# Block 2's norm ahead of the context's masking, and a reordered opening, in a cross-attention and feed-forward kernel

## The chip, the cores and the metric

The kernel runs on one core of a Trainium2 chip. Its engines work at the same time, each through its own queue and in order: TensorE (PE, with weight loads listed as PEld), VectorE (DVE), ScalarE (ACT), GpSimd (POOL), and SyncE (SP), which issues most of the DMAs. [...] The metric is the time of one execution on the device in microseconds (us). Before the change the median of three runs is 1310.03 us (1309.79 to 1311.21).

## The reference, cut to what matters

There is one batch: 2048 rows of `x` with 256 features, a context of 1601 rows with 192 features, 16 heads of 64 and a feed-forward part whose weights are signs. Everything is float32.

```python
xn  = layer_norm(layer_norm(x)) * g_norm
q   = xn @ Wq;   k, v = split(context @ Wkv)
k, v = concat(null_kv[0], k), concat(null_kv[1], v)     # key 0 is the null key
sim = (q / 64**.25) @ (k / 64**.25).T                   # masked keys get -max
att = softmax(sim) @ v
x   = x + layer_norm(att @ Wout) * g_out
h   = relu(s0 * [u, -u] @ (+-1 of k0)) * 2              # u = layer_norm(x)
h   = relu(s1 * h @ (+-1 of k1)) * 2
out = x + s2 * h @ (+-1 of k2)
```

## The kernel before, in words

**Units.** The 2048 rows are four blocks of 512 (`b`), the heads eight pairs (`p`). A pair and a block are a unit `u`, 32 in all, pair by pair. A unit has three parts. In the first, 13 steps over chunks of 128 keys (`k`), PE makes scores with the keys on the partitions (`exps`, tile `sT`, L393); for `k` of 0 and 1 it adds minus the row maximum to them (L404), for later `k` it adds the scores with stepped keys (`kT` holds each chunk minus the one two before, `keys_stepped`), so that a tile turns from chunk to chunk. ACT takes the exponential into `e` (L406), and POOL adds the `e` up in `acc` (L621, L623). Between these steps PE and DVE make the row maxima of the next unit: `max_chunk` multiplies rounded queries and keys (`qr`, `kr`, L356), and DVE reduces them (L359). There are 12 chunks, numbered 3t + c (t a group of 128 rows, c one of three groups of 512 keys), and one for the remaining 66 keys (`REST`, L340 and L343). In the second part PE forms the weighted sums (`weighted`, tile `av`, L413, 52 matmuls) and, early in it, the denominators of the unit before (`divided`). In the third part, between units, ACT copies `av`; the maxima, combined by `max_combined` into `mcol` (L364), are turned by PE (`max_turned`, L369) and spread by DVE into `mT` (L371); the output projection of the unit before follows, the queries of the unit after the next (`project_q`, L213, with `qr` and `qT` made by ACT), and a quarter of the next pair's keys or values (`project_k`, `project_v`).

**Norm of the input.** For each block, `input_root` takes statistics on DVE (L77, L78) and the root on ACT (L443); `input_normed` takes the reciprocal and `nm`, the negated mean, on DVE (L447, L140), and then two ACT instructions a group of 128 rows (L143, L144) with `beside`, or DVE alone (L89); `input_turned` transposes on PE (L458, tile `xT`), and ACT and DVE write one half each of `xnT` (L459, L463; for block 1 both halves are ACT's). Blocks 0 and 1 are done in the opening, blocks 2 and 3 in units 0 and 1, between `max_combined` and the weighted sums (L642, L643). Only unit 0, just ahead of that, reloads half of `ctx_b` and multiplies both context tiles with the mask `keep` on DVE (L641): later pairs need them masked. Also in unit 0 DVE prepares the signs and scales of the feed-forward part (L665 to L669).

**The opening** (L468 to L578) is one list written out by hand, and each engine runs its part of it in that order. It has the loads, the norm of block 0, 40 idle matmuls (20 calls, 2 each) ahead of the first transposes, and for pair 0 the keys in four pieces (`first_keys`: matmuls L224 and L225; DVE masks them into `kT`, L227, and writes `kr` with the null key where the mask drops a key, L228), the values (`first_values`, two halves of matmuls, then a copy by ACT, L283), the first queries, the maxima of unit 0, the norm and turning of block 1, and the mask as a bias, `maskb` (L562, L563). The inverse mask `drop` is made on ACT (L530).

**PSUM.** There are two pools of two tiles, each tile two banks: `flex` and `spare`. In the opening and the feed-forward part `slot` takes from them alternately. A tile waits until the last reader of the one it replaces is done. DVE and ACT do not read one PSUM tile at the same time: at both places where they read `xT`, DVE begins when ACT is done.

**Feed-forward part.** After the last unit a block's rows go through three layers. Values are split into a rounded part `hi` (ACT) and the rest `lo` (DVE); `layer_pair` multiplies both with the same weights (L720), `first` and the loop of L774 drive it.

Of the kernel before, what the change touches and what calls it, by code (L numbers as in the profile page):

```python
# [36 lines left out]
def xattn_ffn(ctx, tc, x, ctxT, mask, g_norm, null_kv, wq, wkv, wout, g_out, k0, k1, k2, s0, s1, s2, out):  # L37
# [108 lines left out]
    with ExitStack() as att:  # L146
# [71 lines left out]
        def first_keys(n, get):  # L218

            kT, _, kr = pairs[0]  # L220
            start, w = CHUNKS[n]
            keys = ds(start, w)
            ps = get(f"psk_0_{n}")
            nc.tensor.matmul(ps[:, 0, :w], weights[0][1][:, 0, :], ctx_a[:, keys], start=True, stop=False)  # L224
            nc.tensor.matmul(ps[:, 0, :w], weights[0][2][:, 0, :], ctx_b[:, keys], start=False, stop=True)  # L225

            nc.vector.tensor_tensor(kT[:, keys], ps[:, 0, :w], keep[:, keys], ALU.mult)  # L227
            nc.vector.scalar_tensor_tensor(kr[:, keys], drop[:, keys], nullk[:, 0:1], kT[:, keys], ALU.mult, ALU.add)  # L228
            if n == 0:
# [148 lines left out]
        def rows_of(k):  # L378
            return 128 if k < KC - 1 else KLAST

        def exps(p, b, k, sT):

            kT, qT, mT = pairs[p][0], queries[p, b][0], shifts[p, b]
            n = rows_of(k)
            ps = sT[k % 2]  # L390
            for j in range(2):
                rows = ts(j, DH)
                nc.tensor.matmul(  # L393
                    ps[:n, j, :],
                    kT[rows, ds(128 * k, n)],
                    qT[rows, :],
                    start=k < 2,
                    stop=k >= 2,
                    skip_group_check=k >= 2,
                )  # L400
            if k < 2:
                for j in range(2):
                    rows = ts(j, DH)
                    nc.tensor.matmul(ps[:n, j, :], ones_r[rows, :n], mT[rows, :], start=False, stop=True)  # L404
            e = ep.tile([128, 2, 512], F32, tag="e", name=f"e_{p}_{b}_{k}")
            nc.scalar.activation(e[:n], ps[:n], AF.Exp, bias=maskb[:n, k : k + 1])  # L406
            return e
# [44 lines left out]
                centred(y_sb[:, 4 * b + j, :], x_sb[:, 4 * b + j, :], mv, r, j)  # L452

        def input_turned(b, get=flex):
            pt = get(f"xT_{b}")
            for j in range(4):
                for c in range(2):
                    nc.tensor.transpose(pt[:, c, ts(j, 128)], y_sb[:, 4 * b + j, ts(c, 128)], ident)  # L458
            nc.scalar.mul(xnT[:, b, 0, :], pt[:, 0, :], gn_sb[:, 0:1])  # L459
            if b == 1:  # L460
                nc.scalar.mul(xnT[:, b, 1, :], pt[:, 1, :], gn_sb[:, 1:2])
            else:
                nc.vector.tensor_scalar_mul(xnT[:, b, 1, :], pt[:, 1, :], gn_sb[:, 1:2])  # L463
# [64 lines left out]

        for keys in (ds(0, 512), ds(512, KEYS - 512)):
            nc.scalar.activation(drop[:, keys], keep[:, keys], AF.Identity, bias=ones[:, 0:1], scale=-1.0)  # L530
        input_normed(0, *xn)

        idle = slot("idle")
        for _ in range(20):
            nc.tensor.matmul(idle[:, 0, :128], ident, ident, start=True, stop=True)
        input_turned(0, slot)
        first_keys(0, slot)
        project_q(0, 0, slot)
        xn = input_root(1)
        first_keys(1, slot)  # L540
        input_normed(1, *xn, beside=True)

        nc.scalar.activation(warm, eps_sb, AF.Exp)

        max_chunk(0, 0, 0, slot)
        max_chunk(0, 0, 3, slot)
        first_keys(2, slot)
        max_chunk(0, 0, 6, slot)
        first_values(0, 0, slot)
        max_chunk(0, 0, 9, slot)  # L550
        first_values(0, 1, slot)
        max_chunk(0, 0, 1, slot)
        first_keys(3, slot)
        keys_stepped(0)
        first_values(1, 0, slot)
        max_chunk(0, 0, 4, slot)
        first_values(1, 1, slot)
        max_chunk(0, 0, 7, slot)
        input_turned(1, slot)
        max_chunk(0, 0, 10, slot)  # L560

        nc.vector.tensor_scalar(maskb[:, : KC - 1], mcol_u8[:, : KC - 1], -MASKED, MASKED, ALU.mult, ALU.add)  # L562
        nc.vector.tensor_scalar(  # L563
            maskb[:KLAST, KC - 1 : KC], mcol_u8[:KLAST, KC - 1 : KC], -MASKED, MASKED, ALU.mult, ALU.add
        )
        first_values(2, 0, slot)
        max_chunk(0, 0, 2, slot)
        first_values(2, 1, slot)
        max_chunk(0, 0, REST, slot)
        first_values(3, 0, slot)  # L570
        max_chunk(0, 0, 5, slot)
        project_q(0, 1, slot, 0)
        max_chunk(0, 0, 8, slot)
        max_chunk(0, 0, 11, slot)
        project_q(0, 1, slot, 1)
        max_combined(0, 0)
        max_turned(0, 0)
        begin.__exit__(None, None, None)  # L578
        last = None
        with tc.manual_schedule():  # L580
            for u, (p, b) in enumerate(units):
# [27 lines left out]
                for k in range(KC):  # L609
                    if k == 2 and last is not None:  # L610
                        nc.scalar.copy(seen[:, 1:2], last[3][:1, 0, 0:1])  # L611
                    if k == 0:

                        odd = spare(f"sT_{p}_{b}_1")
                        sT = [spare(f"sT_{p}_{b}_0"), odd]
                    es.append(exps(p, b, k, sT))
                    if nxt is not None:
                        max_chunk(*nxt, order[k])
                    m = rows_of(k)
                    if k == 1:  # L620
                        nc.gpsimd.tensor_tensor(acc, es[0], es[1], ALU.add)  # L621
                    elif k > 1:
                        nc.gpsimd.tensor_tensor(acc[:m], acc[:m], es[k][:m], ALU.add)  # L623
# [6 lines left out]
                if u == len(units) - 2:  # L630
                    norm_begin(0, y_sb, "y")
                    norm_root(0)
                    norm_end(0, y_sb, y_sb, beside=True)

                    nc.scalar.activation(warm, eps_sb, AF.Exp)
                if u == 0:


                    nc.sync.dma_start(out=ctx_b[64:, 1:], in_=ctxT[128:CD, :])
                    for part in (ctx_a, ctx_b):  # L640
                        nc.vector.tensor_tensor(part, part, keep, ALU.mult)  # L641
                if u < 2:  # L642
                    input_normed(u + 2, *input_root(u + 2), beside=True)  # L643
                    nc.scalar.activation(warm, eps_sb, AF.Exp)

                av = spare(f"av_{p}_{b}")
                for k in range(KC):
# [3 lines left out]
                if u in (len(units) - 4, len(units) - 3):  # L651
# [4 lines left out]
                    else:  # L656
# [57 lines left out]
    def layer_pair(b, n, g, out, w, parts, chunks):  # L714

        ps = slot(f"ps{n}_{b}_{g}")
        steps = [(c, part) for c in range(chunks) for part in range(2)]
        for i, (c, part) in enumerate(steps):
            for f in range(2):
                nc.tensor.matmul(  # L720
# [115 lines left out]
```

## Time and profile before

| | us |
|---|---|
| median of three runs | 1310.03 |
| the profiled execution's own time | 1309.9 |
| its span | 1308.1 |
| PE busy | 1290.2 |
| DVE busy | 819.7 |
| POOL busy | 997.9 |
| ACT busy | 624.7 |
| start of the first exponential | 39.21 |
| end of unit 0's weighted sums | 65.02 |
| start of unit 1's first scores | 80.64 |

The page gives the busy time of each engine, the span in 40 slices of 32.7 us (a digit is tenths), the chain of work that ended last, and groups of instructions by line. The list in order of time has a line for each stretch of equal instructions: its start, its duration, engine, line, the operation, `out<-in` with sizes, how many, and in brackets the idle time of the engine ahead of it with what ended that idle time. The table by stretches gives a stretch, its length, the busy time of PE, PEld, DVE, ACT and POOL with numbers of instructions, the granted clock of PE (1.00 is full), and the DMA's share and rate.

### The profile page before, as it was taken

How to read it: one execution, taken by the hardware profiler on the slowest of the kernel's cores; microseconds unless marked ns; L12 is line 12 of the kernel's file. 1: busy time of each engine (PE TensorE's matmuls, PEld its weight loads, DVE VectorE, ACT ScalarE, POOL GpSimd, SP SyncE). 2: the span in 40 equal slices, each digit the busy share in tenths (PEclk: the TensorE clock that was granted, in tenths of full speed). 3: DMA queues.
4: the chain of work that ended last, by engine and by line, in shares of the span. 5: the costliest groups of instructions: out<-in, count | busy, mean ns of one | idle time of the engine just before them, and what ended most of it. 6: DMA issues, size and time to landing. Idle time of an engine off the chain costs nothing.

```text
span 1308.1 us, 15963 instructions
## 1 busy us (share of the span) xinstructions
PE 1290.2 (99%) x6568; PEld 657.8 (50%) x6568; DVE 819.7 (63%) x822; ACT 624.7 (48%) x740; POOL 997.9 (76%) x503
## 2 busy tenths in 40 slices
PE   8989999999999999999999999999999999999998
PEld 6334444444444444444444444444444443688887
DVE  7877666666666666666666666666666784554431
ACT  4576444444444444454555555555555457321121
POOL 4768988898889888998889888988898999611100
PEclk9989999999999999999999999999999999999999
DMA  6100000000000000000000000000000010000000
GB/s 143 21 1 5 1 1 13 6 1 1 13 5 1 1 13 5 1 1 5 9 5 1 1 13 5 1 1 5 1 17 1 1 41 1 1 9 9 17 17 17
DMA packets 16122, 13.18 MB, mean 10 GB/s; under 512 B 2656, under 2 KB 15520, under 8 KB 16048
## 3 DMA queue, kind: packets, MB, share of 16 engines
q1 hardware_dynamic: 14928, 11.02, 3.2%
q8 instruction: 52, 0.85, 0.3%
q10 hardware_dynamic: 640, 0.79, 0.2%
q0 software_dynamic: 480, 0.34, 0.2%
q14 instruction: 22, 0.18, 0.0%
HBM read 10.04 MB, written 2.10 MB: 9 GB/s over the span
## 4 chain that ended last, share of the span: by engine, by line
PE 91%; DVE 3%; ACT 2%; POOL 2%; DMA 1%; issue 1%; SPq 0%; DVEq 0%; POOLq 0%; ACTq 0%
PE sT L393 28%; PE av L413 26%; PE ps L720 9%; PE max L356 7%; PE psq L213 4%; PE po L421 4%; PE ps L746 2%; PE den L431 2%; PE psv L298 2%; PE psk L238 2%; PE sT L404 1%; DVE mx L359 1%; POOL acc L623 1%; PE psv L310 1%; DMA x_sb<-in_x 1%; PE psk L243 1%
## 5 line engine op out<-in xcount | busy, mean ns | idle before, releaser
L623 POOL TENSOR_TENSOR acc<-acc,e 128x1024 f32<-128x1024 f32 (+1 forms) x352 | 847.0, 2406 | 27.6
L359 DVE TENSOR_REDUCE mx<-max 128x2 f32<-128x1024 f32 x384 | 452.0, 1221 | 81.4 <-PE max L356 81.3
L406 ACT ACTIVATE e<-sT,maskb 128x1024 f32<-128x1024 f32 (+1 forms) x416 | 459.6, 1113 | 42.0 <-PE sT L404 11.8
L393 PE MATMUL sT<-qT,kT 64*128 64x512 f32 (+1 forms) x1664 | 448.5, 612 | 0.8 <-ACT e L406 0.2
L413 PE MATMUL av<-e,v 128*64 128x512 f32 (+1 forms) x1664 | 369.5, 594 | 0.2 <-ACT e L406 0.2
L356 PE MATMUL max<-kr,qr 64*128 64x512 f32 x768 | 292.4, 750 | 0.0
L413 PEld LDWEIGHTS av<-e,v 128*64 128x64 f32 (+1 forms) x1664 | 116.7, 137 | 237.7 <-issue 222.6
L393 PEld LDWEIGHTS sT<-qT,kT 64*128 64x128 f32 (+1 forms) x1664 | 130.4, 181 | 153.6 <-ACT e L406 144.3
L671 ACT COPY avs<-av 128x512 f32<-128x512 f32 x32 | 18.7, 585 | 321.6 <-PE av L413 321.6
L433 DVE RECIPROCAL aoT<-den 128x512 f32<-128x512 f32 x31 | 104.0, 3356 | 60.0 <-PE den L431 60.0
L621 POOL TENSOR_TENSOR acc<-e,e 128x1024 f32<-128x1024 f32 x32 | 75.6, 2362 | 70.1 <-ACT seen L611 58.4
L356 PEld LDWEIGHTS max<-kr,qr 64*128 64x128 f32 x768 | 76.1, 187 | 90.4 <-DVE mx L359 68.4
L371 DVE TENSOR_TENSOR mT<-mt,pick 128x512 fp32r<-128x512 f32 x32 | 22.1, 691 | 119.0 <-PE mt L369 119.0
L720 PE MATMUL ps<-h0hi,w 128*128 128x512 f32 x256 | 79.6, 392 | 0.1
L720 PE MATMUL ps<-h0lo,w 128*128 128x512 f32 x256 | 78.9, 389 | 0.0
L122 POOL TENSOR_TENSOR y_sb<-y_sb,gout_sb 128x256 f32<-128x256 f32 x12 | 9.3, 776 | 88.8 <-DVE y_sb L89 88.8
L214 ACT ACTIVATE qr<-psq 128x512 fp32r<-128x512 f32 x32 | 19.1, 597 | 100.0 <-PE psq L213 97.1
L213 PE MATMUL psq<-xnT,wq 128*128 128x512 f32 x124 | 60.2, 609 | 2.5 <-DVE xnT L463 2.5
L709 DVE SCALAR_TENSOR_TENSOR h1lo<-ps,h1hi 128x1024 fp32r<-128x1024 f32 x16 | 19.6, 1224 | 68.3 <-ACT h1hi L708 68.2
L708 ACT ACTIVATE h1hi<-ps 128x1024 fp32r<-128x1024 f32 x16 | 16.4, 1025 | 95.0 <-PE ps L720 95.0
L421 PE MATMUL po<-wo,aoT 128*128 128x256 f32 x256 | 60.6, 379 | 0.0
L404 PE MATMUL sT<-mT,ones_r 64*128 64x512 f32 x128 | 52.3, 787 | 1.3 <-DVE mT L371 1.3
(157 smaller groups left out, 1060.9 us busy)
## 6 DMA issues: line engine op xcount, KB each, us to landing
out_x<-o SPq DMA_DIRECT2D x7, 256.0 KB, 2.1
x_sb<-in_x SPq DMA_DIRECT2D x3, 512.0 KB, 8.2
wa<-in_wkv SPq DMA_DIRECT2D x8, 128.0 KB, 2.7
wq<-in_wq SPq DMA_DIRECT2D x8, 128.0 KB, 2.2
wo<-in_wout SPq DMA_DIRECT2D x8, 128.0 KB, 2.0
xnT<-in_k SPq DMA_DIRECT2D x1, 1024.0 KB, 5.7
wb<-in_wkv SPq DMA_DIRECT2D x15, 64.0 KB, 2.4
ctx_a<-in_ctxT SPq DMA_DIRECT2D x2, 256.0 KB, 8.1
```

The source lines that it names most:

```text
L213: nc.tensor.matmul(ps[:, 0, :], weights[p][0][:, c, :], xnT[:, b, c, :], start=c == 0, stop=c == 1)
L356: nc.tensor.matmul(ps[:, j, :w], qr[rows, ts(t, 128)], kr[rows, ds(start, w)], start=True, stop=True)
L359: nc.vector.tensor_reduce(maxima[p, b][:, t, :, c], ps[:, :, :w], AX.X, ALU.max)
L393: nc.tensor.matmul(ps[:n, j, :], kT[rows, ds(128 * k, n)], qT[rows, :], start=k < 2, stop=k >= 2, skip_group_check=k >= 2,)
L404: nc.tensor.matmul(ps[:n, j, :], ones_r[rows, :n], mT[rows, :], start=False, stop=True)
L406: nc.scalar.activation(e[:n], ps[:n], AF.Exp, bias=maskb[:n, k : k + 1])
L413: nc.tensor.matmul(av[ts(j, DH), 0, :], v[:n, k, ts(j, DH)], e[:n, j, :], start=k == 0, stop=k == KC - 1)
L421: nc.tensor.matmul(pv[:, t, :], aoT[:, ts(t, 128)], weights[p][3], start=True, stop=True)
L433: nc.vector.reciprocal(aoT, ps)
L621: nc.gpsimd.tensor_tensor(acc, es[0], es[1], ALU.add)
L623: nc.gpsimd.tensor_tensor(acc[:m], acc[:m], es[k][:m], ALU.add)
L720: nc.tensor.matmul(ps[:, f, :], w(c)[:, ts(2 * g + f, 128)], parts[part][:, c, :], start=i == 0, stop=i == len(steps) - 1,)
```

## The change

The change has five parts.

1. Unit 0: the norm of block 2 (statistics, root, norm on ACT) stands ahead of the reload and the masking of the context. The sign operations move from unit 0 to unit 2.
2. Rounded keys: for all keys from 512 on, ACT writes the null key's part into `kr` once (one instruction over 1090 keys), and POOL adds `kT` to it piece by piece, where DVE made both in one instruction. `maskb` moves from DVE to POOL and to an earlier place.
3. Order of the opening: 17 calls of idle matmuls instead of 20; block 0's two halves of `xT` in two PSUM tiles; the chunks of maxima in twos; statistics of block 1 behind the third piece of keys, its norm behind chunk 9, the load of the Exp table behind chunk 4; the turning of block 1 behind chunk 10; three tiles near the end taken from a named pool.
4. First scores: `scores` is split from `exps`; unit 0's scores for `k` of 1 are issued ahead of the turning of the maxima, those for `k` of 0 behind it.
5. Feed-forward: in layer 0 the steps are sorted, all `hi` ahead of all `lo`.

```diff
@@ first_keys
-            nc.vector.scalar_tensor_tensor(kr[:, keys], drop[:, keys], nullk[:, 0:1], kT[:, keys], ALU.mult, ALU.add)
             if n == 0:
+                nc.vector.scalar_tensor_tensor(
+                    kr[:, keys], drop[:, keys], nullk[:, 0:1], kT[:, keys], ALU.mult, ALU.add
+                )
                 nc.vector.tensor_copy(kT[:, 0:1], nullk)
+            else:
+                nc.gpsimd.tensor_tensor(kr[:, keys], kr[:, keys].bitcast(F32), kT[:, keys], ALU.add)
@@ exps
-        def exps(p, b, k, sT):
+        def scores(p, b, k, ps):
...
+        def exps(p, b, k, sT):
+            mT = shifts[p, b]
+            n = rows_of(k)
+            ps = sT[k % 2]
+            if (p, b) != (0, 0) or k >= 2:
+                scores(p, b, k, ps)
@@ input_turned
             pt = get(f"xT_{b}")
+            pts = (pt, get("xT_0_1") if b == 0 else pt)
             for j in range(4):
                 for c in range(2):
-                    nc.tensor.transpose(pt[:, c, ts(j, 128)], y_sb[:, 4 * b + j, ts(c, 128)], ident)
-            nc.scalar.mul(xnT[:, b, 0, :], pt[:, 0, :], gn_sb[:, 0:1])
+                    nc.tensor.transpose(pts[c][:, c, ts(j, 128)], y_sb[:, 4 * b + j, ts(c, 128)], ident)
+            nc.scalar.mul(xnT[:, b, 0, :], pts[0][:, 0, :], gn_sb[:, 0:1])
...
@@ opening
+        nc.scalar.mul(pairs[0][2][:, 512:], drop[:, 512:], nullk[:, 0:1])
         input_normed(0, *xn)
         idle = slot("idle")
-        for _ in range(20):
+        for _ in range(17):
             nc.tensor.matmul(idle[:, 0, :128], ident, ident, start=True, stop=True)
         input_turned(0, slot)
         first_keys(0, slot)
         project_q(0, 0, slot)
-        xn = input_root(1)
         first_keys(1, slot)
-        input_normed(1, *xn, beside=True)
-        nc.scalar.activation(warm, eps_sb, AF.Exp)
+        nc.gpsimd.tensor_scalar(maskb[:, : KC - 1], mcol_u8[:, : KC - 1], -MASKED, MASKED, ALU.mult, ALU.add)
...
         max_chunk(0, 0, 0, slot)
         max_chunk(0, 0, 3, slot)
         first_keys(2, slot)
+        xn = input_root(1)
         max_chunk(0, 0, 6, slot)
+        max_chunk(0, 0, 9, slot)
+        input_normed(1, *xn, beside=True)
         first_values(0, 0, slot)
-        max_chunk(0, 0, 9, slot)
         first_values(0, 1, slot)
         max_chunk(0, 0, 1, slot)
+        max_chunk(0, 0, 4, slot)
+        nc.scalar.activation(warm, eps_sb, AF.Exp)
         first_keys(3, slot)
         keys_stepped(0)
         first_values(1, 0, slot)
-        max_chunk(0, 0, 4, slot)
+        max_chunk(0, 0, 7, slot)
         first_values(1, 1, slot)
-        max_chunk(0, 0, 7, slot)
+        max_chunk(0, 0, 10, slot)
         input_turned(1, slot)
-        max_chunk(0, 0, 10, slot)
-        nc.vector.tensor_scalar(maskb[:, : KC - 1], mcol_u8[:, : KC - 1], -MASKED, MASKED, ALU.mult, ALU.add)
...
         first_values(2, 0, slot)
         max_chunk(0, 0, 2, slot)
+        max_chunk(0, 0, REST, slot)
         first_values(2, 1, slot)
-        max_chunk(0, 0, REST, slot)
         first_values(3, 0, slot)
         max_chunk(0, 0, 5, slot)
-        project_q(0, 1, slot, 0)
-        max_chunk(0, 0, 8, slot)
-        max_chunk(0, 0, 11, slot)
-        project_q(0, 1, slot, 1)
+        max_chunk(0, 0, 8, flex)
+        project_q(0, 1, spare, 0)
+        max_chunk(0, 0, 11, flex)
+        project_q(0, 1, spare, 1)
         max_combined(0, 0)
+        odd = spare("sT_0_0_1")
+        sT = [spare("sT_0_0_0"), odd]
+        scores(0, 0, 1, sT[1])
         max_turned(0, 0)
+        scores(0, 0, 0, sT[0])
@@ units
+                if u < 2:
+                    input_normed(u + 2, *input_root(u + 2), beside=True)
+                    nc.scalar.activation(warm, eps_sb, AF.Exp)
                 if u == 0:
                     nc.sync.dma_start(out=ctx_b[64:, 1:], in_=ctxT[128:CD, :])
                     for part in (ctx_a, ctx_b):
                         nc.vector.tensor_tensor(part, part, keep, ALU.mult)
-                if u < 2:
-                    input_normed(u + 2, *input_root(u + 2), beside=True)
-                    nc.scalar.activation(warm, eps_sb, AF.Exp)
...
-                if u == 0:
+                if u == 2:
                     nc.vector.tensor_scalar(sgn, s_sb[:, 0:2], 0.0, None, ALU.is_ge)
@@ layer_pair
         steps = [(c, part) for c in range(chunks) for part in range(2)]
+        if n == 0:
+            steps.sort(key=lambda step: step[1])
```

More of the change, by code (lines that the diff above doesn't have):

```diff
@@ L379, in rows_of @@
             return 128 if k < KC - 1 else KLAST
-        def exps(p, b, k, sT):
-            kT, qT, mT = pairs[p][0], queries[p, b][0], shifts[p, b]
+        def scores(p, b, k, ps):
+            kT, qT = pairs[p][0], queries[p, b][0]
             n = rows_of(k)
-            ps = sT[k % 2]
             for j in range(2):
@@ L455, in input_turned @@
             pt = get(f"xT_{b}")
+            pts = (pt, get("xT_0_1") if b == 0 else pt)
             for j in range(4):
                 for c in range(2):
-                    nc.tensor.transpose(pt[:, c, ts(j, 128)], y_sb[:, 4 * b + j, ts(c, 128)], ident)
-            nc.scalar.mul(xnT[:, b, 0, :], pt[:, 0, :], gn_sb[:, 0:1])
+                    nc.tensor.transpose(pts[c][:, c, ts(j, 128)], y_sb[:, 4 * b + j, ts(c, 128)], ident)
+            nc.scalar.mul(xnT[:, b, 0, :], pts[0][:, 0, :], gn_sb[:, 0:1])
             if b == 1:
-                nc.scalar.mul(xnT[:, b, 1, :], pt[:, 1, :], gn_sb[:, 1:2])
+                nc.scalar.mul(xnT[:, b, 1, :], pts[1][:, 1, :], gn_sb[:, 1:2])
             else:
-                nc.vector.tensor_scalar_mul(xnT[:, b, 1, :], pt[:, 1, :], gn_sb[:, 1:2])
+                nc.vector.tensor_scalar_mul(xnT[:, b, 1, :], pts[1][:, 1, :], gn_sb[:, 1:2])
         units = [(p, b) for p in range(NP) for b in range(NB)]
@@ L538, in xattn_ffn @@
         project_q(0, 0, slot)
-        xn = input_root(1)
         first_keys(1, slot)
-        input_normed(1, *xn, beside=True)
-        nc.scalar.activation(warm, eps_sb, AF.Exp)
+        nc.gpsimd.tensor_scalar(maskb[:, : KC - 1], mcol_u8[:, : KC - 1], -MASKED, MASKED, ALU.mult, ALU.add)
+        nc.gpsimd.tensor_scalar(
+            maskb[:KLAST, KC - 1 : KC], mcol_u8[:KLAST, KC - 1 : KC], -MASKED, MASKED, ALU.mult, ALU.add
+        )
         max_chunk(0, 0, 0, slot)
@@ L555, in xattn_ffn @@
         first_values(1, 0, slot)
-        max_chunk(0, 0, 4, slot)
+        max_chunk(0, 0, 7, slot)
         first_values(1, 1, slot)
-        max_chunk(0, 0, 7, slot)
+        max_chunk(0, 0, 10, slot)
         input_turned(1, slot)
-        max_chunk(0, 0, 10, slot)
-        nc.vector.tensor_scalar(maskb[:, : KC - 1], mcol_u8[:, : KC - 1], -MASKED, MASKED, ALU.mult, ALU.add)
-        nc.vector.tensor_scalar(
-            maskb[:KLAST, KC - 1 : KC], mcol_u8[:KLAST, KC - 1 : KC], -MASKED, MASKED, ALU.mult, ALU.add
-        )
         first_values(2, 0, slot)
         max_chunk(0, 0, 2, slot)
+        max_chunk(0, 0, REST, slot)
         first_values(2, 1, slot)
-        max_chunk(0, 0, REST, slot)
         first_values(3, 0, slot)
         max_chunk(0, 0, 5, slot)
-        project_q(0, 1, slot, 0)
-        max_chunk(0, 0, 8, slot)
-        max_chunk(0, 0, 11, slot)
-        project_q(0, 1, slot, 1)
+        max_chunk(0, 0, 8, flex)
+        project_q(0, 1, spare, 0)
+        max_chunk(0, 0, 11, flex)
+        project_q(0, 1, spare, 1)
         max_combined(0, 0)
+        odd = spare("sT_0_0_1")
+        sT = [spare("sT_0_0_0"), odd]
+        scores(0, 0, 1, sT[1])
         max_turned(0, 0)
+        scores(0, 0, 0, sT[0])
         begin.__exit__(None, None, None)
@@ L611, in xattn_ffn @@
                         nc.scalar.copy(seen[:, 1:2], last[3][:1, 0, 0:1])
-                    if k == 0:
+                    if k == 0 and u > 0:
                         odd = spare(f"sT_{p}_{b}_1")
```

## The prediction

> **What bounds the kernel now.** I read the page's slices first, then the tail of the first unit and the opening in order of time, then the granted clock by stretches. PE is busy for 99% of the span, and the chain that ended last is PE for 91%, so only the places where PE is short of work can give time. The slices show two: the first two tenths, and the last.
>
> ```profile
> PE 1290.2 (99%) x6568; PEld 657.8 (50%) x6568; DVE 819.7 (63%) x822; ACT 624.7 (48%) x740; POOL 997.9 (76%) x503
> PE   8989999999999999999999999999999999999998
> PEclk9989999999999999999999999999999999999999
> ```
>
> The third slice of the clock is lower. That is the end of unit 0, in order of time (start, duration, engine, what, idle before and its releaser):
>
> ```profile
> 55.11 2.88 DVE L641 TENSOR_TENSOR ctx_a<-ctx_a,keep 128x1602 f32<-128x1602 f32 x1
> 57.92 3.98 DVE L641 TENSOR_TENSOR ctx_b<-ctx_b,keep 128x1602 f32<-128x1602 f32 x1
> 64.07 0.30 ACT L443 ACTIVATE rstd_x<-mv_x,eps_sb 128x4 f32<-128x4 f32 x1 [8.14 <-DVE mv_x L78]
> 64.50 2.08 DVE L140 TENSOR_SCALAR nm<-mv_x 128x4 f32<-128x4 f32 x1
> 67.72 0.44 PE L458 MATMUL xT<-ident,y_sb 128*128 128x128 f32 x2 [2.70 <-ACT y_sb L144]
> 73.90 3.78 PE L213 MATMUL psq<-xnT,wq 128*128 128x512 f32 x4 [2.46 <-DVE xnT L463]
> 80.64 1.02 PE L393 MATMUL sT<-qT,kT 64*128 64x512 f32 x4
> ```
>
> The weighted sums end at 65.02, and then PE waits: DVE masks the context first (6.8 us), only then come the statistics of block 2, its norm on ACT, the turning, and the queries. The clock by stretches (busy time of PE, PEld, DVE, ACT, POOL, then PEclk) adds a second cost:
>
> ```profile
> 68.00:71.00 3.00, 1.74 (x8) 0.95 (x7) 2.90 (x4) 2.88 (x7) 2.92 (x2) 0.69 0.00 0
> 71.00:73.90 2.90, 0.44 (x3) 0.04 (x2) 1.24 (x3) 2.05 (x4) 2.75 (x2) 0.50 0.00 0
> 73.90:76.00 2.10, 2.10 (x3) 1.07 (x4) 0.54 (x1) 0.00 (x0) 0.00 (x0) 0.50 0.00 0
> 78.00:80.00 2.00, 2.00 (x6) 0.81 (x6) 0.00 (x0) 0.80 (x2) 0.00 (x0) 0.66 0.00 0
> 80.00:82.00 2.00, 2.00 (x14) 1.17 (x16) 0.60 (x2) 0.97 (x4) 0.00 (x0) 1.00 0.04 8
> ```
>
> The means 0.69 and 0.66 put the fall to one half at about 69.1 and the return at about 79.4. So psq to the first sT takes 6.74 here; in the next unit, at full clock, 3.94 (111.28 to 115.22).
>
> The opening, in order of time:
>
> ```profile
> 11.03 0.69 ACT L459 ACTIVATE xnT<-xT,gn_sb 128x512 f32<-128x512 f32 x1 [1.84 <-DMA gn_sb<-in_g_norm]
> 14.44 0.43 DVE L77 BATCH_NORM_STATS2 st_x<-x_sb 128x6 f32<-128x256 f32 x1 [0.30 <-DMA x_sb<-in_x]
> 18.08 2.35 DVE L359 TENSOR_REDUCE mx<-max 128x2 f32<-128x1024 f32 x2
> 23.48 0.57 ACT L283 COPY v<-psv 128x512 f32<-128x512 f32 x1
> 24.11 0.49 PE L278 MATMUL psv<-wa,ctx_a 128*128 128x128 f32 x2 [0.45 <-ACT v L283]
> 36.78 0.19 DVE L364 TENSOR_REDUCE mcol<-mx 128x8 f32<-128x32 f32 x1
> 39.21 1.11 ACT L406 ACTIVATE e<-sT,maskb 128x1024 f32<-128x1024 f32 x1 [2.46 <-PE sT L404]
> ```
>
> From 14.44 to 36.78 DVE is nearly full: it is the opening's bound. ACT norms block 1 from 18.20 to 22.08 (3.88), loads the Exp table, and only then copies the first values; PE waits for that copy at 24.11.
>
> **The change, part by part.** Times are against the first exponential (39.21), called e0.
>
> Unit 0's tail. Before: mcol at e0+15.8, psq at e0+34.7, first sT of unit 1 at e0+41.4. After: the second score pair is already made and the third starts sooner, 0.3 off (the third reduction at e0+2.9 before, about e0+2.5 then), so mcol at 15.5 and the end of the weighted sums at 25.5 instead of 25.8. Statistics 2.3, root 0.3, reciprocal 0.15: nm is asked for at 18.45. It waits for POOL: in the trace nm, ctx_a and ctx_b each start real work only where an acc ends (nm asked at 64.50, done 66.58; acc every 2.44). With POOL's steps counted from e0+2.3, nm is done at 19.4 (18.5 to 20.9 by phase). ACT norms 3.88 to 23.3, table and warm 1.48 to 24.8: all beside PE's weighted sums. xT 25.5 to 26.6 (1.04), xnT's first half on ACT to 27.3. DVE masks after nm: one acc, 1.7 us of ctx_a, one acc, 1.7 us of ctx_b, done at 27.6; the second half of xnT waits for it until 28.3, and the masks are in time for psk at 30.1. psq at 28.4, with the full clock (PE idles 1.5) sT at 32.3. **Gain 9.1**: about 6.3 of waiting, 2.8 of clock. With nm at its latest the masks end at 29.0, psq is at 29.8, the gain 7.7; without the waits for POOL 9.5. POOL's acc ends at e0+34.4, before unit 1 looks for it at 35.1, so nothing new waits. The sign operations (L665 to L669, 4.9 us here, finished at 71.4 before DVE was asked at 73.09) cost DVE the same in unit 2 between aoT (139.05) and mT: mT slips from 143.47 to about 144.5, needed by PE at 150.04: nothing. If that cover were gone, up to 4.9.
>
> The opening's start. Three idle matmuls fewer: 1.06 less, transposes at 8.9 instead of 9.62. gn_sb still lands at 11.03, so of that 0.4 reaches psq (11.8 for 12.22). Two tiles let DVE's half of xnT start at 11.03 instead of 11.75; kT0 starts at 11.9 for 12.47. The new product on ACT (1090 keys) is priced by the drop row of that length, 1.19, in the 1.84 wait for gn_sb, nullk having landed at 9.5: nothing; at twice that price +1.0. The keys on POOL: 128x256 takes 0.73, 128x1024 2.36, so 512 is 1.3 (between these); kr1 is ready at 17.5 and asked for at 21.0, kr2 at 20.5 and 31.5, so even 2.36 is hidden. DVE loses two times 0.75, 0.29 and 0.41 for maskb: 2.2. maskb on POOL (two of 0.3, the ones_r row) is hidden in POOL's idle 11 us. The block-1 statistics no longer wait for x_sb (14.41).
>
> The opening's middle. I followed each engine in the order of the code with the rows' durations (max pair 0.43 on PE, 1.17 on DVE; values 1.08 a half; keys 1.78; a PSUM tile is taken when the earlier freed of its pool's two is free). For the order of before this gives mcol at 36.80; the trace has 36.78. For the new order: kT1 at 15.5, first reduction 16.2 (18.08), statistics 19.2 to 21.4, the reductions of chunks 6 and 9 to 23.7, nm only then; ACT norms from 24.0 to 27.9, so the copy of the first values, behind it in ACT's queue, is at 27.9 instead of 23.48. What is late next: the second values start at 26.3, after chunk 4's reduction frees a tile, instead of 24.11; max 7 stands behind them on PE, and DVE idles 1.5, then 0.3, 1.4 and 0.8. mcol comes at 38.2: **+1.4**, although DVE has 2.2 less to do. If the second values get the tile that the first values hold (each pool's two in turn), they start at 28.45 and the sum is +3.7; the trace fits both, since before tiles came free in the order in which they were taken. I take +1.4, the freer tile. mcol to e0 stays 2.4: the scores moved ahead run under mcol and mT.
>
> The clock in the opening. Between 21.4 and 26.3 PE then has 0.9 us of work (idle 1.2, 0.7 and 2.1). In the trace a stretch of 3.4 us before 69.1 (a third of the 10.2 between fall and return) with 0.88 busy ended in the fall, one with 60% busy (72.6 to 76.0) did not bring it back, a full one did. If the fall comes here at 24.9 to 26.8 and the return 3.4 to 6.8 later, PE, the bound from 26.3 on, loses 1.3 to 3.0; no fall, 0. I take **+2.1**, since 25% busy is what fell. [...]
>
> The feed-forward. Sorting the steps takes PE's wait for ulo (0.53 at 1121.47) down by 0.45 in block 0, but layer 1 then waits for h0lo, which starts where POOL's acc ends:
>
> ```profile
> 1121.47 0.73 PE L720 MATMUL ps<-ulo,w 128*128 128x512 f32 x2 [0.53 <-DVE ulo L134]
> 1127.44 4.62 DVE L709 SCALAR_TENSOR_TENSOR h0lo<-ps,h0hi 128x1024 fp32r<-128x1024 f32 x4 [4.90 <-POOL acc L623]
> ```
>
> So 0 (at best -0.45); later blocks make uT a layer ahead. Without that cover the gain would show, not a loss.
>
> Sum: -9.1 + 1.4 + 2.1 = -5.6. The profiled execution took 1309.9 (span 1308.1), 0.1 under the median of 1310.03; so 1304.3 in its terms, 1304.4 as a median.
>
> **The rivals.**
> No fall of the clock in the opening: 1310.0 - 9.1 + 1.4 = 1302.3. For it: idle times are short, each with work between; against it: 69.1.
> Tiles in turn: 1310.0 - 9.1 + 3.7 + 2.1 = 1306.7.
> Masks late: nm just misses an acc, gain 7.7: 1305.8. For it: 2.08 at 64.50; against: the phase counted above.
> The opening shortens as DVE's load does, the norm of block 1 blocking nothing: mcol 2.8 earlier, 1298.1. Against it: PE's wait for ACT's copy at 24.11.
> The slower side: the half clock, once fallen at 25, stays through the opening because PE waits between its pieces. PE's 13 us of work from 26.3 on then take 26: 1310.0 - 9.1 + 1.4 + 13 = 1315.3; it decides once the clock's loss passes 7.7, a half clock until about 41.7. For it: 72.6 to 76.0 was 60% busy and stayed low; against: PE's queue from 26.3 on has no gap.
>
> **How the numbers follow.** Forecast 0.36; no fall 0.24; tiles in turn 0.15; masks late 0.11; opening shorter 0.05; slower side 0.09. A change of 0.2% (2.6 us) is about what a measurement of this kernel tells from none. The first four lie beyond it, save a third of tiles in turn; slower is the last case: faster 0.86, same 0.05, slower 0.09. The forecast's own range is 1303.0 (gain 9.5, clock 1.3) to 1305.9 (8.4, 3.0). The range runs from 1301.0 (no fall, gain 9.5, order +0.5, should chunk 7 reach DVE 0.9 sooner) to 1308.0 (tiles in turn, gain 9.1, clock 3.4, order +3.7); the last two cases, 0.14, stay outside.
>
> **What would show it.** xT of block 2 right where the weighted sums end, psq within 3 us of that, PEclk 1.00 to the first sT: tail right. ACT's first copy of values near 28 and DVE idle before chunk 7: middle right. PEclk below 1 between 25 and 33: clock right. mcol before 36.8, or a first exponential after 46, makes the prediction wrong; so does psq waiting on ctx_b.

## The result, and the profile after

The changed kernel takes 1305.02 us (median of 6 runs, 1303.46 to 1306.38), the kernel before, run beside it, 1310.26 (6 runs, 1308.82 to 1311.21). The ratio is 0.996, with a 95% interval from 0.9947 to 0.9973: 5.2 us less, where 1304.4 in all, 5.6 less, was forecast. The profiled execution has a span of 1303.2 us for 1308.1, so 4.9 less; the steps below are summed against that.

The busy times and the slices of the page after, in the form of those shown of before:

```profile
PE 1288.7 (99%) x6562; PEld 658.5 (51%) x6562; DVE 817.4 (63%) x817; ACT 625.9 (48%) x741; POOL 1001.9 (77%) x508
PE   8999999999999999999999999999999999999998
PEclk8999999999999999999999999999999999999999
```

Before, the third slice of PE and of the clock was low (unit 0's end). Now, beside PE's last, only the first is: unit 0's end is mended, and the opening's clock is worse. The end of unit 0 after, in order of time (start, duration, engine, line, what, and in brackets the idle time ahead and its releaser):

```profile
58.25 0.19 DVE L369 TENSOR_REDUCE mcol<-mx 128x8 f32<-128x32 f32 x1
61.02 0.87 DVE L140 TENSOR_SCALAR nm<-mv_x 128x4 f32<-128x4 f32 x1
61.81 1.81 DVE L663 TENSOR_TENSOR ctx_a<-ctx_a,keep 128x1602 f32<-128x1602 f32 x1
63.55 3.99 DVE L663 TENSOR_TENSOR ctx_b<-ctx_b,keep 128x1602 f32<-128x1602 f32 x1
68.18 1.09 PE L471 MATMUL xT<-ident,y_sb 128*128 128x128 f32 x8
70.84 1.98 PE L213 MATMUL psq<-xnT,wq 128*128 128x512 f32 x4 [1.46 <-DVE xnT L476]
74.88 1.02 PE L391 MATMUL sT<-qT,kT 64*128 64x512 f32 x4
```

PE turns block 2 (xT) with no wait behind the weighted sums, and psq waits 1.46 us; before, xT waited 2.70 us and psq 2.46. psq to the first sT takes 4.04 us for 6.74, at full clock. The first exponential (e0 again) is at 42.66, so the first sT of unit 1 is at e0+32.22; before it was at e0+41.43. That is 9.2 us less.

The opening after, the same columns:

```profile
16.54 2.35 DVE L364 TENSOR_REDUCE mx<-max 128x2 f32<-128x1024 f32 x2
16.77 1.27 POOL L235 TENSOR_TENSOR kr<-kr,kT 128x512 fp32r<-128x512 f32 x1 [2.93 <-DVE kT L227]
23.85 0.14 DVE L140 TENSOR_SCALAR nm<-mv_x 128x4 f32<-128x4 f32 x1
26.30 0.79 PE L283 MATMUL psv<-wa,ctx_a 128*128 128x128 f32 x2 [1.74 <-DVE mx L364]
27.79 0.57 ACT L288 COPY v<-psv 128x512 f32<-128x512 f32 x1
29.14 1.23 DVE L364 TENSOR_REDUCE mx<-max 128x2 f32<-128x1024 f32 x1 [2.77 <-PE max L361]
40.58 0.19 DVE L369 TENSOR_REDUCE mcol<-mx 128x8 f32<-128x32 f32 x1
42.66 2.12 ACT L417 ACTIVATE e<-sT,maskb 128x1024 f32<-128x1024 f32 x2 [1.73 <-PE sT L415]
```

The first reduction is 1.5 us earlier than before and mcol 3.8 us later. Between them DVE, full before, idles 2.8 us at 26.4 and PE waits. The table by stretches (stretch, length, busy time of PE, PEld, DVE, ACT, POOL with instructions, then the granted clock, DMA share and rate), cut where the clock turns:

```profile
22.25:25.66 3.41, 1.16 (x6) 0.71 (x6) 3.41 (x6) 1.57 (x4) 0.00 (x0) 1.00 0.02 5
25.66:29.07 3.41, 2.77 (x11) 2.11 (x11) 0.72 (x2) 3.33 (x7) 0.57 (x2) 0.50 0.00 0
29.07:32.48 3.41, 3.41 (x16) 2.75 (x15) 1.84 (x2) 1.38 (x3) 3.10 (x5) 0.50 0.00 0
```

PE is busy for 1.16 of 3.41 us, then its clock is one half until 32.48, just when it has much to do. In the tail the same view shows no fall:

```profile
68.00:71.00 3.00, 1.54 (x12) 1.13 (x11) 0.96 (x2) 1.27 (x2) 2.92 (x2) 1.00 0.00 0
71.00:73.00 2.00, 2.00 (x6) 0.90 (x6) 0.38 (x1) 0.14 (x1) 1.92 (x2) 1.00 0.01 4
```

Two small losses come behind it. As unit 1 starts, DVE's rounded keys of the next pair (L255) take 2.39 us. In the kernel before the same two instructions took 1.18 (the last line; its POOL sum had ended at 73.83):

```profile
69.84 7.21 POOL L642 TENSOR_TENSOR acc<-acc,e 128x1024 f32<-128x1024 f32 x3
75.65 2.39 DVE L255 SCALAR_TENSOR_TENSOR kr<-drop,nullk,kT 128x401 fp32r<-128x401 uint8 x2 [4.27 <-ACT kT L254]
79.22 0.51 PE L361 MATMUL max<-kr,qr 64*128 64x512 f32 x2 [0.45 <-DVE mx L364]
81.40 1.18 DVE L250 SCALAR_TENSOR_TENSOR kr<-drop,nullk,kT 128x401 fp32r<-128x401 uint8 x2 [6.96 <-ACT kT L249]
```

POOL's running sum of unit 0 ends at 77.05; the keys end only at 78.0, the maxima behind them are late, and PE waits for them. First scores to weighted sums of unit 1 last 16.34 us (74.88 to 91.22), before 15.70: 0.64 lost. In unit 2 the sign operations, moved there, take 7.1 us (4.9 in unit 0 before), and the spreading of the maxima, mT, starts only at 141.00:

```profile
133.89 2.31 DVE L684 TENSOR_SCALAR sgn<-s_sb 128x2 f32<-128x2 f32 x1
136.45 2.20 DVE L686 TENSOR_TENSOR s_sb<-s_sb,sgn 128x2 f32<-128x2 f32 x1
138.93 2.15 DVE L688 TENSOR_TENSOR s_out<-s_out,s_sb 128x1 f32<-128x1 f32 x1
141.00 0.68 DVE L376 TENSOR_TENSOR mT<-mt,pick 128x512 fp32r<-128x512 f32 x1
```

The products of the next pair's values start 0.15 us later behind the queries' and take 2.05 us for 1.95; the unit lasts 34.62 us for 34.36: about 0.25 lost. From unit 3 on both traces run at a constant distance, 4.90 us, to the end. The sum: 3.45 (e0) - 9.2 + 0.64 + 0.25 = -4.9.

### The profile page after: what moved, and what is told of

The parts are those of the page before. It is cut to its first block, busy times and chain, and to the rows that moved or that the text cites. A ratio compares the mean times of both kernels' runs of the same rounds, so it can differ in the third digit from the quotient of the medians.

```text
span 1303.2 us, 15959 instructions
## 1 busy us (share of the span) xinstructions
PE 1288.7 (99%) x6562; PEld 658.5 (51%) x6562; DVE 817.4 (63%) x817; ACT 625.9 (48%) x741; POOL 1001.9 (77%) x508
## 4 chain that ended last, share of the span: by engine, by line
PE 94%; DVE 2%; POOL 2%; ACT 1%; issue 0%; DVEq 0%; POOLq 0%; ACTq 0%
PE sT L391 29%; PE av L424 27%; PE ps L742 10%; PE max L361 7%; PE psq L213 4%; PE po L432 4%; PE ps L768 2%; PE den L442 2%; PE psv L303 2%; PE psk L243 1%; PE sT L415 1%; POOL acc L642 1%; PE psv L315 1%; PE psk L248 1%; PE max L345 1%; DVE mx L364 1%
## 5 line engine op out<-in xcount | busy, mean ns | idle before, releaser
L742 PEld LDWEIGHTS ps<-h0lo,w 128*128 128x128 f32 x256 | 48.0, 188 | 10.1
```

The lines of the kernel that those rows point to most:

```text
L742: nc.tensor.matmul(ps[:, f, :], w(c)[:, ts(2 * g + f, 128)], parts[part][:, c, :], start=i == 0, stop=i == len(steps) - 1,)
```

## The experiments

No kernel here leaves out any of the computation. The kernel before was run beside each batch; its medians there were 1309.87, 1309.48, 1310.14 and 1309.64, so kernels of different batches are compared by their ratios.

**The parts, one at a time.** The tail alone, in the kernel before:

```diff
+                if u < 2:
+                    input_normed(u + 2, *input_root(u + 2), beside=True)
+                    nc.scalar.activation(warm, eps_sb, AF.Exp)
                 if u == 0:
                     nc.sync.dma_start(out=ctx_b[64:, 1:], in_=ctxT[128:CD, :])
                     for part in (ctx_a, ctx_b):
                         nc.vector.tensor_tensor(part, part, keep, ALU.mult)
-                if u < 2:
-                    input_normed(u + 2, *input_root(u + 2), beside=True)
-                    nc.scalar.activation(warm, eps_sb, AF.Exp)
...
-                if u == 0:
+                if u == 2:
                     nc.vector.tensor_scalar(sgn, s_sb[:, 0:2], 0.0, None, ALU.is_ge)
```

> Only unit 0's tail is changed (norm of block 2 ahead of the masking, sign operations in unit 2); the opening is that of before. Theory: the tail gives 9.2 us from the first exponential to unit 1's first scores, unit 1 gives back 0.6 to 0.7 (its first keys wait for POOL) and unit 2 0.2, so -8.0 to -8.3 against before: about 1302.1, some 3 us below the full change. The first exponential stays at 39.2. Rival (the opening's parts help, or cost nothing): the full change is as fast as this or faster, so this would take 1305 or more.

Measured: 1302.85 (1301.71 to 1304.94), ratio 0.9944 (0.9932 to 0.9957). The tail carries the gain. By the ratio it is 7.3 us (5.6 to 8.9) where 8.0 to 8.3 was expected. In the profiled execution the clock fell in another place, right behind the first exponential:

```profile
36.65:40.06 3.41, 1.71 (x13) 1.03 (x11) 1.57 (x4) 0.94 (x2) 0.00 (x0) 1.00 0.01 3
40.06:43.46 3.40, 3.40 (x18) 2.22 (x16) 1.36 (x2) 1.42 (x3) 1.38 (x1) 0.50 0.00 0
```

PE waits there for the maxima (0.42 us) and for mT (1.27 us). The kernel before has the same waits in the same place (0.42 and 1.26) and kept the full clock in its profile. The first sT of unit 1 is then at e0+33.99, 1.77 later than after the whole change: about half of 3.4 us. Against the expectation, unit 1 lost nothing here (15.71 us from first scores to weighted sums): with the tail later, DVE's keys began at e0+34.8, only 0.4 us ahead of the end of POOL's sum, and took 1.41 us. Of the five executions the slowest had the lowest mean granted clock (1304.94 us, 0.997) and the fastest the highest (1301.71, 1.000).

The opening alone, the changed kernel with unit 0's tail put back:

```diff
-                if u < 2:
-                    input_normed(u + 2, *input_root(u + 2), beside=True)
-                    nc.scalar.activation(warm, eps_sb, AF.Exp)
                 if u == 0:
...
+                if u < 2:
+                    input_normed(u + 2, *input_root(u + 2), beside=True)
+                    nc.scalar.activation(warm, eps_sb, AF.Exp)
...
-                if u == 2:
+                if u == 0:
                     nc.vector.tensor_scalar(sgn, s_sb[:, 0:2], 0.0, None, ALU.is_ge)
```

> The full change with the masking back ahead of block 2's norm and the sign operations back in unit 0: the opening and the sorted first layer alone. Theory: the first exponential comes at 42.6 instead of 39.2, the tail has its 15.6 us from the end of the weighted sums to the first scores and its half clock again: +3.1 to +3.5 against before, about 1313.5. Rival (the opening gains and the tail alone is over-counted): 1310 or less.

Measured: 1312.24 (11 runs, 1311.4 to 1314.29), ratio 1.0016 (1.0007 to 1.0025): 2.1 us slower (2.4 by the medians). The other parts of the change cost time, as forecast, but less than the 3.1 to 3.5 expected: in this profile the half clock lasted from 26.98 to 30.39 and not for two such stretches, and e0 came at 41.55.

**Does the thin stretch let the clock fall?** A first try put idle matmuls into PE's waiting places, written into the second bank of the tile of the first values:

```diff
+        def fill(n):
+            for _ in range(n):
+                nc.tensor.matmul(halves[0][:, 1, :128], ident, ident, start=True, stop=True)
...
         max_chunk(0, 0, 1, slot)
+        fill(3)
         max_chunk(0, 0, 4, slot)
+        fill(1)
...
+        fill(4)
         first_values(1, 0, slot)
```

> The full change with 8 calls (16 instructions) of 128-wide matmuls of the identity put into PE's three waits between 21.4 and 26.3 us, into an unused half of the first values' PSUM tile: nothing but PE's idle time is taken. Theory: the granted clock stays at 1.00 through the opening, PE's work from 26.3 to 32.5 runs in its usual time, the first exponential comes 2.4 earlier (40.3), the whole is 2.4 below the full change: about 1302.6. Rival (the half clock is hidden behind DVE or ACT in the opening): clock 1.00, but the first exponential within 0.5 of 42.7, time as the full change, 1305.

Measured: 1310.22 (11 runs), ratio 0.9999 (0.999 to 1.0007): neither. The edit made a wait of its own:

```profile
28.21 1.65 PE L562 MATMUL psv<-ident 128*128 128x128 f32 x6 [6.87 <-ACT v L288]
```

The fill writes into a tile that ACT has yet to copy, so PE stood still from 21.3 to 28.2. This run says nothing on the question. The second try writes into tiles that PE has just taken and that nobody reads yet:

```diff
@@ first_keys
+            if n == 3:
+                fill(ps, 4)
             nc.tensor.matmul(ps[:, 0, :w], weights[0][1][:, 0, :], ctx_a[:, keys], start=True, stop=False)
@@ max_chunk
             start, w = CHUNKS[c]
+            if (p, b) == (0, 0):
+                fill(ps, {1: 3, 4: 2}.get(n, 0))
```

> The changed kernel with idle matmuls put into PE's waiting places of the opening, this time written into tiles that PE has just taken and no other engine reads yet: 3 ahead of chunk 1's products, 2 ahead of chunk 4's, 4 ahead of the last piece of keys (0.35 us each, 3.2 us in all, where PE idles 1.2, 0.6 and 1.7 us). Theory (the thin stretch from 21.4 to 26.3 is what lets the clock fall at 25.7, and the fall costs 2.4 us): the clock stays 1.00 from 17 to 33 us, the first exponential comes at 40.3 for 42.66, time about 1302.6. Rival (the clock falls here whatever PE does): half clock again from about 25 to 32, first exponential 42.7 to 43, time 1305.0 to 1305.5.

Measured: 1302.11 (1301.93 to 1302.61), ratio 0.9942 (0.9927 to 0.9957), 2.4 us under the changed kernel's ratio. The clock stays whole in the same stretches:

```profile
22.25:25.66 3.41, 2.62 (x18) 2.06 (x18) 3.41 (x6) 2.16 (x5) 0.00 (x0) 1.00 0.00 0
25.66:29.07 3.41, 3.35 (x23) 2.63 (x24) 1.57 (x4) 3.33 (x6) 1.07 (x4) 1.00 0.00 0
29.07:32.48 3.41, 3.41 (x33) 2.99 (x31) 2.05 (x2) 1.96 (x5) 3.10 (x5) 1.00 0.00 0
```

The first exponential is at 39.57, 3.09 earlier than in the profile after; 0.58 of it was already there at the statistics of block 1 (18.81 for 19.39). So the clock is 2.5 of the 3.45 that the opening lost, and the order 0.9, by one execution of each. Work that computes nothing made the kernel faster. To see how much is needed, the same without the four ahead of the last keys:

```diff
@@ first_keys
-            if n == 3:
-                fill(ps, 4)
```

> As the run with all idle matmuls, but only the 3 ahead of chunk 1's products and the 2 ahead of chunk 4's; PE's wait of 1.74 us ahead of the second values stays. It asks what lets the clock fall. If it is the mean load of the stretch, 63% from 21.4 to 26.3 us instead of 28%: the clock stays 1.00, time within 0.6 us of 1302.1. If a single wait of 1.7 us is enough: half clock from about 25 us again, first exponential 2 us later than in that run, time 1304.0 to 1305.0.

Measured: 1303.68 (1302.98 to 1304.99), ratio 0.9956 (0.9939 to 0.9972). That is between the two cases: 1.8 us over the full fill by the ratios, and the first exponential at 40.73 for 39.57. The clock fell, behind the wait of 1.74 us, for one stretch:

```profile
23.91:27.32 3.41, 1.74 (x12) 1.38 (x13) 1.86 (x4) 3.31 (x8) 0.00 (x0) 1.00 0.00 0
27.32:30.72 3.40, 3.40 (x15) 2.74 (x15) 2.07 (x2) 2.29 (x4) 2.70 (x6) 0.50 0.00 0
```

The mean over 21.4 to 26.3 was the wrong measure: in the 3.41 us up to the fall PE was busy for 51%. By itself this run would also fit the other reading, that one wait of 1.7 us is enough. Two other runs speak for the share: a stretch whose longest wait was 0.94 us (PE busy for 47%, next run) ended in a fall, and one with a wait of 1.45 us (57%, the tail of the run with keys from PSUM) did not.

**The copy of the first values.** The norm of block 1 stands behind the first values in ACT's queue, not ahead:

```diff
-        input_normed(1, *xn, beside=True)
         first_values(0, 0, slot)
         first_values(0, 1, slot)
+        input_normed(1, *xn, beside=True)
```

> The full change with the norm of block 1 behind the first values in the code, so that ACT copies the first values ahead of the norm's eight instructions. Theory (that copy is what held PE and with it the maxima, and PE's waits let the clock fall): the second values start at 24.2 instead of 26.3, the combined maxima come at about 36.8 instead of 40.6, the first exponential at about 39.2, clock 1.00; the whole 3.4 below the full change, about 1301.6. Rival (the lost time is the late statistics on DVE, whatever stands ahead in ACT's queue): the combined maxima stay at 40 or later and the time at 1304 to 1305.

Measured: 1302.2 (1300.81 to 1304.73), ratio 0.9941 (0.9927 to 0.9954). The copy is at 21.68 for 27.79, mcol at 37.81 for 40.58, the first exponential at 39.90, 0.7 later than expected, with a half clock from 24.86 to 28.27 all the same. The late statistics on DVE are not the cause, since they stayed (19.23 for 19.39). ACT's queue, with PE behind it, is what made the order cost time: directly, and by one more stretch of half clock.

**The rounded keys.** Back on DVE, without ACT's product and POOL's sums:

```diff
-            if n == 0:
-                nc.vector.scalar_tensor_tensor(kr[:, keys], drop[:, keys], nullk[:, 0:1], kT[:, keys], ALU.mult, ALU.add)
...
-                nc.gpsimd.tensor_tensor(kr[:, keys], kr[:, keys].bitcast(F32), kT[:, keys], ALU.add)
+            nc.vector.scalar_tensor_tensor(kr[:, keys], drop[:, keys], nullk[:, 0:1], kT[:, keys], ALU.mult, ALU.add)
```

> The changed kernel with the rounded keys of the opening back on DVE in one instruction each (two of 0.72 us and one of 0.29), without ACT's product and POOL's sums. Theory (up to 26 us DVE is full and sets the opening): the two early ones push everything behind them, the first exponential comes 1.2 to 1.7 us later, time 1306.2 to 1306.7, so that moving the keys is what keeps the new order from costing more. Rival (DVE idles 2.8, 1.5, 1.5 and 0.6 us behind 26 us, which takes them up): first exponential within 0.4 us of 42.66, time 1304.9 to 1305.4.

Measured: 1306.95 (9 runs, 1305.47 to 1310.53), ratio 0.9976 (0.9966 to 0.9987), 2.1 us over the changed kernel's ratio. The move is worth its place. The median is a little above the theory's span; why is not shown, since the profiled execution is the slowest of the nine (1310.53): there the half clock lasted 10.24 us (26.37 to 36.61), the first exponential came at 45.84, and the clock fell once more in the tail.

**The loss in unit 1.** The keys of pair 1's first half read one operand from PSUM:

```diff
                 nc.scalar.copy(kT[:, keys], ps[:, i, :w])
-                nc.vector.scalar_tensor_tensor(kr[:, keys], drop[:, keys], nullk[:, 0:1], kT[:, keys], ALU.mult, ALU.add)
+            for i in range(2):
+                keys = ds(start + i * w, w)
+                added = ps[:, i, :w] if (p, m) == (1, 0) else kT[:, keys]
+                nc.vector.scalar_tensor_tensor(kr[:, keys], drop[:, keys], nullk[:, 0:1], added, ALU.mult, ALU.add)
```

> The changed kernel with one operand of the rounded keys of pair 1's first half read from PSUM (the tile of the products) instead of SBUF, and both of ACT's copies ahead of them. Theory (in unit 0's third part DVE's two key instructions take 2.39 us instead of 1.18 because, with both operands in SBUF, they wait for the end of POOL's running sum, and unit 1 loses 0.64 us by it): the two take about 1.2 us, the weighted sums of unit 1 start about 15.7 us after its first scores for 16.34, time 1304.4 to 1304.6. Rival (the wait is not POOL's; the maxima of unit 1 wait for PE or ACT anyway): the two stay at 2.4 us or the start of the weighted sums stays at 16.3, time 1305.0.

Measured: 1304.05 (1303.69 to 1305.53), ratio 0.9959 (0.9944 to 0.9973). The ratio can't tell 0.5 us; the trace can:

```profile
70.33 7.22 POOL L643 TENSOR_TENSOR acc<-acc,e 128x1024 f32<-128x1024 f32 x3
76.52 1.18 DVE L258 SCALAR_TENSOR_TENSOR kr<-drop,nullk,psk 128x401 fp32r<-128x401 uint8 x2 [4.66 <-ACT kT L254]
```

POOL's sum runs until 77.55, over the same instructions, and they take 1.18 us. First scores to weighted sums: 15.80 us for 16.34. So the 2.39 held about 1.2 us of waiting for POOL, and with one operand in PSUM there was none. Why the place of one operand decides that, no run here shows.

**The feed-forward part.** The sort of the first layer's steps taken out:

```diff
         steps = [(c, part) for c in range(chunks) for part in range(2)]
-        if n == 0:
-            steps.sort(key=lambda step: step[1])
```

> The changed kernel with the steps of the feed-forward part's first layer unsorted again, as before. Theory (PE's wait for ulo is shorter by the sort, but layer 1 waits for h0lo, which waits for the end of POOL's last running sum): layer 1 starts at the same distance from the last unit's first scores, time as the changed kernel, 1305.0 within 0.2. Rival (the sort saves the wait for ulo): 0.45 slower, 1305.4 to 1305.5.

Measured: 1303.97 (1303.87 to 1304.96), ratio 0.9956 (0.9941 to 0.9971). The time is 1 us under the span expected, but not by the edit: the first exponential was already 1.00 earlier in its profile (41.66). From the last unit's weighted sums to layer 1 it is 23.48 us with the sort out (1099.17 to 1122.65), 23.49 with it, and 23.47 in the kernel before. The sort is worth nothing, as forecast.

**The repairs together.**

```diff
@@ project_k
+                added = ps[:, i, :w] if (p, m) == (1, 0) else kT[:, keys]
@@ max_chunk
+                fill(ps, {1: 3, 4: 2}.get(n, 0))
@@ opening
-        input_normed(1, *xn, beside=True)
         first_values(0, 0, slot)
         first_values(0, 1, slot)
+        input_normed(1, *xn, beside=True)
@@ units
+                if u == 2:
+                    nc.vector.tensor_scalar(sgn, s_sb[:, 0:2], 0.0, None, ALU.is_ge)
...
                 av = spare(f"av_{p}_{b}")
```

> The changed kernel with four repairs together: the copy of the first values ahead of block 1's norm in ACT's queue, idle matmuls in PE's waiting places ahead of chunks 1 and 4 (3 and 2), the rounded keys of pair 1's first half from PSUM, and the sign operations of unit 2 ahead of its weighted sums, in DVE's wait for the denominators. Theory: 2.8 (as measured alone for the first) + 1.6 (the clock's loss that was left there) + 0.6 + 0.2 off 1305.0: about 1299.8; from unit 3 on a constant distance of about 10.1 us to the kernel before. Rival (the clock falls all the same, or its fall moves behind the first exponential): 1301.3 to 1301.8.

Measured: 1300.61 (1299.85 to 1301.0), ratio 0.9929 (0.9915 to 0.9944). The mean granted clock of the profiled execution is 1.000, e0 at 37.56. But unit 2 now takes 35.23 us, more than the 34.62 of the change: in one piece ahead of the reciprocal the sign operations make aoT, the divided sums, 0.61 us late for PE. The next kernel splits them:

```diff
                 if u == 2:
                     nc.vector.tensor_scalar(sgn, s_sb[:, 0:2], 0.0, None, ALU.is_ge)
                     nc.vector.tensor_scalar(sgn, sgn, 2.0, -1.0, ALU.mult, ALU.add)
+                if u == 3:
                     nc.vector.tensor_tensor(s_sb[:, 0:2], s_sb[:, 0:2], sgn, ALU.mult)
+                if u == 4:
                     nc.vector.tensor_scalar(s_out, s_sb[:, 0:1], s_sb[:, 1:2], 8.0, ALU.mult, ALU.mult)
                     nc.vector.tensor_tensor(s_out, s_out, s_sb[:, 2:3], ALU.mult)
                 av = spare(f"av_{p}_{b}")
```

> The four repairs, with the sign operations split over units 2, 3 and 4 (two, one and two of them), each ahead of the weighted sums in DVE's wait of 2.1 us for the denominators. Theory (in one piece there they made aoT 0.6 us late for PE, so that unit 2 took 35.23 us where it takes 34.36 without them; in pieces nothing is late): units 2, 3 and 4 as long as in the kernel before (34.36 for unit 2), 0.9 off 1300.6: about 1299.7. Rival (each piece waits for POOL's running sum and is late by itself): unit 2 at 34.6 or more, time 1300.2 to 1300.8.

Measured: 1299.86 (1299.42 to 1300.13), ratio 0.9923 (0.9908 to 0.9938). Unit 2 takes 34.37 us, 0.86 less; the intervals of the last two ratios overlap, so this gain is read from the trace. It is the fastest of all kernels here, 4.8 us under the changed one by the ratios. Last, the same tail with the opening of before: the kernel before with the norm ahead of the masking, the keys of pair 1's first half from PSUM and the split sign operations.

> The kernel before with its own opening, the norm ahead of the masking, the rounded keys of pair 1's first half from PSUM, and the sign operations split over units 2, 3 and 4: the repaired tail without the new opening. Theory (the new opening, once the clock no longer falls in it, has its first exponential 1.1 to 1.6 us earlier than the old one): 0.2 to 0.3 under the tail alone (1302.85) where the clock falls behind the first exponential as it did there, 1302.6; without that fall 1300.9; in both cases above the 1299.9 of the four repairs. Rival (the new opening is worth nothing even then): 1299.9 or less.

Measured: 1301.09 (1300.91 to 1304.63), ratio 0.9935 (0.9918 to 0.9951). Three times lie between 1300.91 and 1301.13, the case forecast for a clock that doesn't fall. The fourth, 1304.63, is the profiled one, and its clock fell twice:

```profile
35.63:39.04 3.41, 1.72 (x8) 0.49 (x7) 2.31 (x4) 1.08 (x2) 0.00 (x0) 1.00 0.44 81
39.04:42.45 3.41, 3.41 (x16) 2.10 (x16) 1.23 (x1) 1.19 (x2) 0.00 (x0) 0.50 0.00 0
66.34:69.76 3.42, 1.97 (x14) 1.16 (x11) 1.00 (x2) 1.27 (x2) 3.34 (x2) 1.00 0.00 0
69.76:73.17 3.41, 3.41 (x5) 1.33 (x5) 0.34 (x1) 0.00 (x0) 3.33 (x2) 0.50 0.00 0
```

Two falls of 3.41 us, half of each lost, are 3.4 us, nearly the whole distance of 3.6 to the other three. The mean granted clock fits: 0.997 here, 1.000, 0.999 and 1.000 there. The repaired new opening is then worth 1.2 us by the medians, 1.6 by the ratios, whose intervals overlap; the first exponentials, 38.14 in the best kernel and 39.25 with the tail alone, say 1.1.

## Why the prediction was right, and where it was not

- **Unit 0's tail, -9.1 forecast, -9.2 measured.** The negated mean was done at e0+19.2 for 19.4, xT came where the weighted sums end, psq at e0+28.2 for 28.4, the first sT at 32.2 for 32.3, at full clock. The masks were done at e0+24.9, 2.7 earlier than counted: ctx_a did not wait for POOL, and the step of POOL's sum beside it took 3.91 us for 2.35. So the second half of xnT did not wait for the masks, as the working had it, but for ACT's half (until e0+27.4); the two differ by 0.2, so psq came when forecast all the same.
- **The opening's start.** ACT's product took 1.20 us (1.19) inside the wait for gn_sb, POOL's sums 1.27 each (1.3): hidden, as said. gn_sb landed at 11.45 here, not at 11.03; the 0.4 that fewer idle matmuls were to give went there. Nor did they give 1.06: the 34 took 6.86 us where the 40 took 7.09, and the transposes began at 9.39, not at 8.9.
- **The opening's middle, +1.4.** The copy of the first values came at 27.79 (27.9 forecast), the second values on PE at 26.30 (26.3), released by chunk 4's reduction. So the freer tile was taken, and tiles in turn (28.45) is refuted. By the run with the clock held, the order costs 0.9, in one execution.
- **The clock, +2.1.** It fell at 25.66 (24.9 to 26.8 forecast) and came back 6.8 later (3.4 to 6.8); it cost 2.5 (1.3 to 3.0). e0 moved by 3.45 in all for 3.5, and that closeness is luck in part: the order came out 0.5 cheaper and the clock 0.4 dearer, and with this same opening e0 was 41.66 in the run without the sort and 43.15 in the one with keys from PSUM. The slower side, a half clock that stays to 41.7, did not come: 10.24 us was the longest in any profile.
- **The wrong rival.** No fall at all was argued from idle times that are short, each with work between. The longest wait ahead of the fall was 1.74 us, and the clock fell; the fill, which only adds work, kept it at 1.00. In these profiles PE's share of work in a stretch tells more (0.34 ahead of the fall, 0.77 with the fill; table below).
- **The step that failed: "so nothing new waits".** POOL's running sum was compared with its reader in unit 1 (e0+35.1), not with DVE's key instruction at e0+33.0, which shares no data with it and ended behind it all the same (2.39 us beside the sum, 1.18 behind it in the kernel before): 0.64.
- **The term that was mis-sized:** the sign operations in unit 2 were put at 4.9 us and at nothing on the path; they took 7.1 us and cost about 0.25. Three of the five last about 2.2 us, nearly a step of POOL's sum (2.36).
- **Feed-forward, 0:** right, and for the reason given.

The two missed terms come to 0.9; the tail and the opening came out 0.15 better than forecast, which leaves the 0.7 between -5.6 and the -4.9 of the profile. The median, -5.2, lies between.

## What to carry to other kernels

Here a stretch in which PE was only partly busy (1.16 of 3.41 us) was followed by half clock (0.50): read the granted clock in such a stretch, and count what keeps PE busy, even idle matmuls in tiles that nobody waits for, as worth a price (they gave 2.4 us here, by the ratios). When work on DVE is moved in time, lay it beside what POOL does then, not only beside what needs its result: DVE's two key instructions took 2.39 us beside POOL's sum and 1.18 behind it. Where there is a choice, try an operand from PSUM (1.18 us beside the sum). An instruction put ahead in one engine's queue (ACT's norm) delayed what another engine waited for behind it (the copy, at 27.79 us; at 21.68 with the norm behind it).

## What the runs showed of the hardware

**In these profiles the clock changed by stretches of 3.41 us.** Between 15 and 82 us, eleven profiles, the kernel before among them, have 14 times of half clock. Seven last 3.4 us, two 6.8, five 10.2: one, two or three stretches. Three of the profiles have two falls each, 30.72, 44.37 and 47.79 us apart: 9, 13 and 14 stretches. Cutting each trace into such stretches, counted from where its clock fell, gives PE's busy share in the stretch ahead:

| PE's share in a stretch at full clock | stretches | then half clock |
|---|---|---|
| 0.23 to 0.51 | 12 | 12 |
| 0.57 to 0.59 | 8 | 2 |
| 0.70 and more | all others | 0 |

A line of the eight, from the table by stretches of the kernel before, ahead of its first exponential:

```profile
34.99:38.40 3.41, 2.00 (x7) 0.44 (x5) 2.42 (x4) 1.08 (x2) 0.00 (x0) 1.00 0.55 98
```

2.00 of 3.41 is 0.59, and the clock stayed. In the two runs with the same opening (the tail alone and the last one) the stretches were cut a little elsewhere over the same waits, the shares were 0.50, and it fell. So in these three profiles the same waits cost clock (0.50) or not (0.59) with the place where they lay in a stretch. At half clock, shares of 0.81 and less never brought the full clock back (10 stretches); a full stretch did in 14 of 16 cases. Why two full ones did not stays open. The tail of the changed kernel had 0.76 in its profile, but 0.57 in six other runs with the same tail, where it fell twice. What parts these two from the other four is not shown; the share is the same.

**Small instructions waited for a large one on another engine.** The sign operations work on 128 x 2 numbers; of the five in unit 2, three took 2.31, 2.20 and 2.15 us beside POOL's sum and two about 0.2. Each of the three ended 0.02 or 0.03 us behind a step of that sum (steps end at 136.18, 138.63 and 141.06). In the best kernel, split, the first three took 1.30, 0.17 and 1.23.
